# Raw weight pieces in three down products, output steps at a third of the chunks, and six banks for the first scores

## The chip, the cores and the metric

One core of a Trainium2 chip runs the whole program. The metric is device time in microseconds (us), the median of several executions. The profile comes from one further execution that the hardware profiler recorded. Engines are named as in the profile: PE is the matrix engine (TensorE) and PEld its weight loads, DVE is VectorE, ACT is ScalarE, POOL is GpSimd and SP is SyncE. SPq and POOLq are the queues on which SP and POOL issue DMAs.

## The reference, cut to what matters

The input is x of shape (2, 2048, 1024) in float32: 4096 rows of 1024.

```python
x = x + attn(layernorm(x))                # one head of width 256, softmax over 2048 keys
n = layernorm(x)
w = sum of the two largest of n @ gate_w  # one number for each row
h = relu(n @ up_w) ** 2                   # 1024 -> 2048
shared = h @ down_w                       # 2048 -> 1024
routed = (n @ fc1_w @ expert_w * w) @ fc2_w   # 1024 -> 512 -> 512 -> 1024
x = x + layernorm(shared + routed) * gamma + beta
```

Everything is float32. The kernel folds `expert_w @ fc2_w` into one matrix, so that the routed path is a second, narrower pair of products beside up and down.

## The kernel before, in words

**Arithmetic.** Every float32 operand is split into a high and a low part (`fp32r`[...]). One product is then three matmuls: high by high, low by high, high by low (`Pass3`, line 117). A split costs one ACT cast (the high part) and one DVE subtraction (the low part).

**Attention.** The rows are handled in eight blocks n of 512. `scores(n, k)` (line 545) makes one 128 by 512 tile of scores with six matmuls into one PSUM bank, for each of sixteen key chunks k. ACT copies the bank to SBUF (line 557), then DVE takes the running maximum from the same bank (line 562), and after both the bank is free. All scores take their bank from the pool `psb`, which has two. The pool `psa` has four: the query, key and value products before the scores use it, and after them the value products `po` (two banks at a time) and the output projection `pw`. The scores of block 0 stand at the end of the projection stage, where nothing else is left for PE. The following loop runs scores of block n beside the value products of block n-1, `lag` chunks behind. For n = 1 that lag is LAG + 2 = 5, so that five scores of block 1 come ahead of the first value product. A scheduler sets the order of instructions in that part of the program.

**Feed-forward.** From here on the order is written out by hand. The up and down products are done with a fast scheme of seven products in place of eight on half-matrices, for four blocks b of 1024 rows. The products of the down stage run in the order p1, p2, p6, p5, p3, p7, p4 (`DOWN`). Each has NK = 10 chunks, and a chunk takes one weight piece and twelve matmuls. The weight pieces of all stages go through one pipeline, `stage`, `cast_piece`, `end_piece`, seven buffers deep:

- a raw piece is a DMA of 256 KB of float32 (SP, line 808), an ACT cast (line 825) and a DVE subtraction (line 833);
- a kept piece is a DMA of 512 KB of both parts (SP, line 805), with no work for ACT or DVE;
- a piece becomes kept when the split buffer is written to DRAM, 512 KB, by a DMA on POOL (line 836).

The rule is that in block 0 every second piece is written, in block 1 the others are, and a piece that has been written is read back as kept from the next block on. The last LATE = 5 pieces of block 3 are loaded early into other buffers (`load_early`) and have to be kept ones.

The left operand of the down stage goes through a like pipeline (`sum_s`, `cast_s` at line 1062, `end_s` at line 1067, with four buffers `sp`): one ACT cast and one DVE subtraction for each chunk, in every block.

**Output.** A finished row tile y (128 by 1024) goes through `out_step` (line 994), which moves each tile waiting there by one step: load the residual into `res` (SP), add beta to it with a DMA (POOL), take the first moment, then the second moment (ACT), then `write` (two long DVE operations, lines 986 and 987, and the store on POOL, line 988). `out_step` is called by hand: in the up stage after every odd m below 15, in the down stage after every even chunk of p7 and after chunks 0 and 2 of p4. The four tiles that p3 finishes are handled during p7 and p4 of the same block, those that p4 finishes in the next block's up stage. Block 3 handles its own last four tiles at the end.

All engines take their instructions in order, so an instruction that waits holds up all behind it on its engine. In the down stage ACT sees, chunk by chunk, the cast of a weight piece and then the cast of a left operand. DVE sees the two subtractions in the same order, with `write`, the evictions of finished products (lines 1255, 1257, 1259) and the splits of the next block's input (line 150) among them. POOL's queue holds the writes of kept pieces, the stores, the beta additions and the transposed tiles of the next norm.

Of the kernel before, what the change touches and what calls it, by code (L numbers as in the profile page):

```python
# [25 lines left out]
def kernel(  # L26
# [47 lines left out]
    psa = ctx.enter_context(tc.tile_pool(name="psa", bufs=4, space=PSUM))  # L74
    psb = ctx.enter_context(tc.tile_pool(name="psb", bufs=2, space=PSUM))
# [17 lines left out]
    def bank(pool, name):  # L93
        return pool.tile([P, W], FP, tag="b", name=name)
# [259 lines left out]
    NK = (NIC + NLC) // 2  # L354
# [177 lines left out]
        return t  # L532

    st = {}

    def kv_home(j):
        return ex_unit if j < 2 * BPB - 1 else unit
# [7 lines left out]
    def scores(n, k):  # L545
        s = st[n]
        if k % 4 == 0:
            s["s"].append(unit(f"s{n}_{k // 4}", FP))
        pm = bank(psb, "ps")
        acc = Pass3(pm, NDC)  # L550
        kk, q = hl(kv_chunk(n, 0, k)), hl(s["q"])
        for dc in range(NDC):
            acc.add(
                tuple(kk[:, i, ds(dc * W + (k % 4) * P, P)] for i in range(2)),
                tuple(q[:, i, ts(dc, W)] for i in range(2)),
            )
        nc.scalar.copy(s["s"][k // 4][:, ts(k % 4, W)], pm)  # L557
        if k == 0:
            s["max"] = half(f"max{n}")
            nc.scalar.copy(s["max"], pm)  # L560
        else:
            nc.vector.tensor_tensor(s["max"], pm, s["max"], ALU.max)  # L562
# [142 lines left out]

    g_f = half("g_f")[:, : NCC * NE].rearrange("p (c e) -> p c e", c=NCC)
    nc.gpsimd.dma_start(out=g_f, in_=gate_w.rearrange("(c p) e -> p c e", p=P))
    LAG = 3
    xts = []
    for n in range(1, NBLK + 1):  # L710
        if n == NBLK:
# [3 lines left out]
        for k in range(NKC + lag):  # L715
# [7 lines left out]
            if k >= lag:  # L723
                values(n - 1, k - lag)
                if n == BPB and (k - LAG) % 4 == 3:
                    j = BPB + (k - LAG) // 4
# [62 lines left out]
    LATE = 5  # L789
# [5 lines left out]
    def stage():  # L795


        b, s, p, i = pieces.pop(0)
        if len(pieces) < LATE and early:
            staged.append((early.pop(0), False, None))  # L800
            return
        n_w[0] += 1
        w = (wk if n_w[0] % 7 else wv).tile([P, 2 * W], FR, tag="w", name="w")
        if (s, p, i) in kept:
            nc.sync.dma_start(out=w.bitcast(FP), in_=kept[s, p, i])
            staged.append((w, False, None))
            return
        nc.sync.dma_start(out=as_piece(f32(w)[:, W : 2 * W], s), in_=source(s, RIGHT[p], i))

        staged.append((w, True, (s, p, i) if b == 1 or i % 2 == 0 else None))  # L810

    early, n_w = [], [0]

# [146 lines left out]
    class Out:  # L960
# [22 lines left out]
        def write(self):  # L983
            y, rs = self.y, self.m.inverse()
            stt = nc.vector.scalar_tensor_tensor
            stt(y, y, self.m.nm, gamma_sb, ALU.add, ALU.mult)
            stt(y, y, rs, self.res, ALU.mult, ALU.add)
            nc.gpsimd.dma_start(out=of[ds(self.n * W + self.t * P, P), :], in_=y)

    res_pair, todo, loaded, first, second = [], [], [], [], []

    def out_step():

        if second:
            second.pop(0).write()
        if first:
            second.append(first.pop(0))
            second[-1].second()  # L1000
        if loaded:
            first.append(loaded.pop(0))
            first[-1].add_beta()
            first[-1].first()
        if todo:
            loaded.append(Out(*todo.pop(0)))
# [11 lines left out]
    with tc.manual_schedule():  # L1018
        for b in range(NBB):
# [72 lines left out]
            for m, (p, i) in enumerate(UPS[b]):  # L1092
                flush()
                w = next_piece()
                if p != "p2":
                    acc[i] = Pass3(acc_bank("pu"), NCC // 2)
                ps = acc[i].ps
                if p == "p2":
                    acc[i].more()
                for c in range(NCC // 2):  # L1100
                    acc[i].add(piece(w, c, P, slice(0, P)), piece(X[p], c, W, slice(0, W)))
                lat, pair = i >= HU // P, i % 2 and i < HU // P
                c22, c21 = h_at("22", i), h_at("21", i) if m >= 2 * NK else None
                if p == "p1":
                    nc.scalar.copy(c22, ps)
                elif p == "p2":
                    if lat:
                        add(h_at("11", i), ps, rwb[0], ALU.mult)
                    else:
                        relu(h_at("11", i), ps)  # L1110
                        if pair:
                            square(h_at("11", i, 2))
                elif p == "p4":
                    nc.scalar.copy(c21, ps)
                elif p == "p6":
                    add(c22, ps, c22, ALU.subtract)
                    add(c21, c21, c22, ALU.subtract)
                elif p == "p5":
                    add(c22, c22, ps, ALU.add)
                elif p == "p3":  # L1120
                    c12 = h_at("12", i)
                    add(c12, c22, ps, ALU.add)  # L1122
                    if lat:
                        add(c12, c12, rwb[0], ALU.mult)
                    elif pair:
                        relu(h_at("12", i, 2), h_at("12", i, 2))
                        square(h_at("12", i, 2))
                else:
                    add(c21, c21, ps, ALU.add)
                    add(c22, c22, ps, ALU.subtract)  # L1130
                    if lat:
                        add(c21, c21, rwb[1], ALU.mult)
                        add(c22, c22, rwb[1], ALU.mult)
                    elif pair:
                        for v in ("21", "22"):
                            relu(h_at(v, i, 2), h_at(v, i, 2))
                            square(h_at(v, i, 2))

                if m % 2 and m < 15:
                    out_step()  # L1140
                if b == 0 and m in (0, 1, 2, 4, 6, 8, 9, 10, 11, 12, 13):
                    norm2.step()
                if b == 0 and m < NB:
                    split_x(x_t[0], 1, m, X["p2"], split_late)

                m4 = 12 if b == 0 else 10
                if m == m4:
                    x_t[1] = norm2.x
                    X["p4"] = new_x()
                if m > m4 and (m - m4) % 2 and (m - m4) // 2 < NB:  # L1150
                    split_x(x_t[1], 1, (m - m4) // 2, X["p4"], split_late)
                elif m >= 2 * NK and p != "p7":
                    n = {"p4": "p6", "p6": "p5", "p5": "p3", "p3": "p7"}[p]
                    if i == 1:
                        X[n] = new_x()
                    if i % 2 and i < 2 * NB:
                        if p == "p4":
                            sums_x(x_t, i // 2)
                        r_, f_ = PLACE[n]
                        split_x(x_t[r_], f_, i // 2, X[n], split_late)  # L1160

                if (p, i) == ("p1", 0 if b else 4):
                    ga = half("ga")[: 2 * NE, :]
                    nc.scalar.copy(ga, gate_part(X["p1"], 0))
                elif (p, i) == ("p2", 0):
                    gs = half("gs")[: 2 * NE, :]
                    add(gs, ga, gate_part(X["p2"], 1), ALU.add)
                    gt = Gate(gs)
                elif (p, i) == ("p4", 1):
                    add(ga, ga, gate_part(X["p4"], 1), ALU.add)  # L1170
                elif (p, i) == ("p7", 0):
                    add(ga, ga, gate_part(X["p7"], 0), ALU.subtract)
                    gt = Gate(ga)
                if m == 6 or (p, i) == ("p7", 3):
                    gt.largest()
                elif m == 10 or (p, i) == ("p7", 6):
                    rwb[p == "p7"] = gt.spread()
                if p == "p7" and i >= NK - 5:
                    step_s()
# [16 lines left out]
            for j, p in enumerate(("p1", "p2", "p6", "p5", "p3", "p7", "p4")):  # L1196
# [12 lines left out]
                for k in range(NK - late):  # L1209
# [19 lines left out]
                    elif not more and j == 4 and k % 2 == 0 and k < 2 * LATE:  # L1229
                        load_early(k // 2)  # L1230
                        if k < 2 * NB:
                            tiles[k // 2].add_beta()
                    if j == 5 and k % 2 == 0 or j == 6 and k in (0, 2):
                        out_step()
                if late:
                    last_w = [next_piece() for _ in range(late)]
# [5 lines left out]
                for t in range(NB):  # L1242
# [17 lines left out]
                    if late:  # L1260
                        tiles[t].first()
                        tiles[t].second()
                        if t:
                            tiles[t - 1].write()
                if late:
                    tiles[-1].write()
                if p == "p3":
                    ended(0)
                elif p == "p4" and not late:
                    ended(1)  # L1270
            if more:
                t1 = norm1.x
        while todo or loaded or first or second:
            out_step()


# [41 lines left out]
```

## Time and profile before

| | us |
|---|---|
| median of 3 runs | 2368.88 (2367.68 to 2369.89) |
| the profiled execution | 2368.2 |
| its span, first to last instruction | 2366.3 |
| down stage, block 0 (976.62 to 1174.92) | 198.30 |
| down stage, block 1 (1374.92 to 1571.18) | 196.26 |
| down stage, block 2 (1771.18 to 1964.22) | 193.04 |
| down stage, block 3 (2164.22 to the end of its last matmul, 2354.78) | 190.56 |
| first score to first value product (309.99 to 344.73) | 34.74 |

The stage bounds are read off the timeline of PE: the start of the first matmul of a kind to the start of the first of the next. A down stage has 7 products of 10 chunks of 12 matmuls, 840 in all, in every block. The profile's own figure for a matmul (390 ns) overlaps its neighbours, so starts are compared and not sums of durations.

The transfers of the whole program, from the page (kind of transfer, count, size, and the median time from issue to landing):

```profile
w<-w_p SPq DMA_DIRECT2D x350, 512.0 KB, 3.7
w_p<-w POOLq DMA_DIRECT2D x140, 512.0 KB, 4.9
w<-wt SPq DMA_DIRECT2D x210, 256.0 KB, 3.7
```

The first line is the loads of kept pieces, the second the writes that make pieces kept, the third the loads of raw pieces.

### The profile page before, as it was taken

The page shows a single profiled execution, that of the slowest core. Times are in us where ns is not written, and L with a number is a line of the kernel's source. Part 1 is how long each engine was busy: PE and PEld are TensorE (multiplying, and loading weights), DVE is VectorE, ACT ScalarE, POOL GpSimd, SP SyncE. Part 2 cuts the span into 40 slices and gives each one's busy share as a digit, 9 for nine tenths or more (in the row PEclk, how much of TensorE's full clock was granted, in tenths as well). Part 3 has the DMA queues.
Part 4 walks back from the last instruction along what each step waited for, and adds up shares of the span by engine and source line. Part 5 has one row for each costly group of instructions (what it writes and reads, how often), then busy time and mean ns, then how long its engine had stood idle before and what let it go on. Part 6 is the DMA issues. An engine that isn't in the chain of part 4 may idle for free.

```text
span 2366.3 us, 29281 instructions
## 1 busy us (share of the span) xinstructions
PE 2329.5 (98%) x10704; PEld 1918.7 (81%) x10704; DVE 1461.0 (62%) x2168; ACT 1131.6 (48%) x1846; POOL 298.4 (13%) x450
## 2 busy tenths in 40 slices
PE   8999999999999999999999999999999999999998
PEld 7888878888888778888778888878888877888886
DVE  5566559888877565797646567644446562435545
ACT  6555445555544644667452374544055454214224
POOL 3222111011110100111110011210000010000001
PEclk9999999999999999999999999999999999999999
DMA  5977883999997765788996689997557798555595
GB/s 189 322 254 278 285 205 114 290 316 320 283 268 213 258 205 183 236 275 270 313 319 231 234 295 332 323 339 238 192 198 270 254 339 290 195 194 187 200 314 188
DMA packets 225806, 603.98 MB, mean 255 GB/s; under 512 B 18768, under 2 KB 80720, under 8 KB 223616
## 3 DMA queue, kind: packets, MB, share of 16 engines
q1 hardware_dynamic: 152160, 334.02, 40.4%
q0 software_dynamic: 73504, 268.11, 37.0%
q8 instruction: 85, 1.39, 0.2%
q14 instruction: 57, 0.47, 0.1%
HBM read 448.96 MB, written 210.76 MB: 279 GB/s over the span
## 4 chain that ended last, share of the span: by engine, by line
PE 90%; DMA 4%; issue 3%; DVE 2%; ACT 1%; POOL 0%; SPq 0%; POOLq 0%; DVEq 0%; ACTq 0%
PE pu L130 31%; PE pd L130 26%; PE po L130 7%; PE pq L130 7%; PE ps L130 7%; PE pw L130 4%; PE pv L130 4%; PE pg L882 1%; PE pf L130 1%; DMA w<-wt 1%; DMA w<-w_p 1%; DMA res<-in_L_ffn_ln_beta_dram 1%; DMA w_p<-w 1%; PE psum L619 1%; DVE w L833 0%
## 5 line engine op out<-in xcount | busy, mean ns | idle before, releaser
L130 PE MATMUL pd<-w,sp 128*128 128x512 f32 x3336 | 762.4, 390 | 11.3 <-DVE sp L1067 7.2
L130 PEld LDWEIGHTS pd<-w,sp 128*128 128x128 f32 x3336 | 626.0, 188 | 146.5 <-DVE sp L1067 10.3
L130 PE MATMUL pu<-xh,w 128*128 128x512 f32 x2240 | 692.9, 390 | 0.1
L130 PEld LDWEIGHTS pu<-xh,w 128*128 128x128 f32 x2240 | 419.4, 188 | 89.6 <-DVE w L833 1.3
L130 PE MATMUL pu<-xl,w 128*128 128x512 f32 x1120 | 436.2, 389 | 0.9 <-DVE xl L150 0.9
L130 PEld LDWEIGHTS pu<-xl,w 128*128 128x128 f32 x1120 | 210.3, 188 | 45.2 <-DVE xl L150 1.4
L1062 ACT CAST sp<-h 128x512 fp32r<-128x512 f32 x238 | 145.9, 618 | 191.5 <-PE pd L130 159.2
L1067 DVE TENSOR_TENSOR sp<-h,sp 128x512 fp32r<-128x512 f32 x238 | 162.1, 686 | 101.3 <-ACT sp L1062 101.0
L825 ACT CAST w<-w 128x512 fp32r<-128x512 f32 x210 | 128.1, 617 | 174.5 <-DMA w<-wt 158.6
L130 PE MATMUL ps<-q,k 128*128 128x512 f32 x768 | 196.0, 393 | 2.0 <-DVE max L562 1.8
L833 DVE TENSOR_TENSOR w<-w 128x512 fp32r<-128x512 f32 x210 | 143.2, 686 | 82.6 <-ACT w L825 81.6
L130 PE MATMUL po<-p,v 128*128 128x512 f32 x768 | 194.2, 391 | 0.0
L130 PEld LDWEIGHTS ps<-q,k 128*128 128x128 f32 x768 | 142.3, 188 | 36.5 <-DVE max L562 7.3
L130 PEld LDWEIGHTS po<-p,v 128*128 128x128 f32 x768 | 143.1, 188 | 29.2
L150 DVE TENSOR_TENSOR xl<-xt,xh 128x512 fp32r<-128x512 f32 x108 | 74.3, 688 | 130.7 <-ACT xh L149 130.6
L1012 ACT ACTIVATE h<-h 128x1024 f32<-128x1024 f32 x48 | 50.6, 1055 | 209.0 <-DVE h L1122 160.0
L836 POOL DMA_DIRECT2D w_p<-w x140 | 75.2, 537 | 564.0 <-DVE w L833 484.4
L557 ACT COPY s<-ps 128x512 f32<-128x512 f32 x128 | 74.8, 584 | 142.0 <-PE ps L130 141.4
L213 DVE STREAM_TRANSPOSE xblk<-xrow 128x1024 f32<-128x1024 f32 x60 | 121.0, 2016 | 9.6 <-ACT xrow L283 9.6
L562 DVE TENSOR_TENSOR max<-ps,max 128x512 f32<-128x512 f32 x120 | 82.0, 684 | 39.5 <-ACT s L557 39.3
L130 PE MATMUL pq<-xha,w_h 128*128 128x512 f32 x256 | 99.7, 389 | 0.0
L130 PE MATMUL pq<-xha,w_l 128*128 128x512 f32 x256 | 99.7, 389 | 0.0
(181 smaller groups left out, 3027.8 us busy)
## 6 DMA issues: line engine op xcount, KB each, us to landing
w<-w_p SPq DMA_DIRECT2D x350, 512.0 KB, 3.7
w_p<-w POOLq DMA_DIRECT2D x140, 512.0 KB, 4.9
w<-wt SPq DMA_DIRECT2D x210, 256.0 KB, 3.7
xt_d<-xblk POOLq DMA_DIRECT2D x56, 512.0 KB, 4.5
xt<-xt_d POOLq DMA_DIRECT2D x56, 512.0 KB, 6.6
wt<-in_L_ffn_up_w_dram POOLq DMA_DIRECT2D x9, 2048.0 KB, 25.8
wt<-in_L_ffn_down_w_dram POOLq DMA_DIRECT2D x9, 2048.0 KB, 35.2
xres<-in_L_attn_x_dram SPq DMA_DIRECT2D x32, 512.0 KB, 12.8
```

What stands on the lines that cost most here:

```text
L130: nc.tensor.matmul(self.ps, lhsT=a, rhs=b, start=self.i == 0, stop=self.i == self.n - 1, skip_group_check=self.on,)
L150: late_ops.append(lambda: nc.vector.tensor_tensor(lo, t, f32(hi), ALU.subtract))
L213: nc.vector.transpose(b.rearrange("p (q k i) -> p q k i", q=P // SQ, i=SQ), r.rearrange("p (k i q) -> p q k i", k=NCC, i=SQ),)
L557: nc.scalar.copy(s["s"][k // 4][:, ts(k % 4, W)], pm)
L562: nc.vector.tensor_tensor(s["max"], pm, s["max"], ALU.max)
L619: nc.tensor.matmul(pt[:, t : t + 1], lhsT=s["sum"][:, ds(i * W + t * P, P)], rhs=ones, start=i == 0, stop=i == 1,)
L825: nc.scalar.copy(w[:, 0:W], f32(w)[:, W : 2 * W])
L833: nc.vector.tensor_tensor(w[:, W : 2 * W], v[:, W : 2 * W], v[:, 0:W], ALU.subtract)
L836: nc.gpsimd.dma_start(out=kept[key], in_=w.bitcast(FP))
L1012: nc.scalar.activation(o, v, AF.Relu)
L1062: nc.scalar.copy(t[:, 0:W], v)
L1067: add(t[:, W : 2 * W], v, f32(t)[:, 0:W], ALU.subtract)
```

## The change

Three edits, independent of each other.

1. In the down stage the pieces of p3, p7 and p4 are not kept any more: they are loaded raw and split anew in each block. The exception is the last five pieces of p4, which are written once in block 2 and loaded early in block 3, as before.
2. The store of a finished row tile is taken out of `write` and made by `out_step` one step later, so that a tile passes through one step more. In the down stage of blocks 0 to 2 `out_step` is called at every third chunk of p7 and p4 taken together (chunks 0, 3, 6, 9 of p7 and 2, 5, 8 of p4). In block 3 it stays at every second, with chunk 4 of p4 added. In the up stage it is called for odd m below 17.
3. The scores of block 0, and the first five of block 1, take two of every three banks from `psa`, so that they rotate over six.

```diff
-        pm = bank(psb, "ps")
+        wide = n == 0 or n == 1 and k < LAG + 2
+        pm = bank(psa if wide and k % 3 else psb, "ps")
...
-        staged.append((w, True, (s, p, i) if b == 1 or i % 2 == 0 else None))
+        if s == 1 and p in ("p3", "p7", "p4"):
+            keep = b == 2 and p == "p4" and i >= NK - LATE
+        else:
+            keep = b == 1 or i % 2 == 0
+        staged.append((w, True, (s, p, i) if keep else None))
...
             stt(y, y, rs, self.res, ALU.mult, ALU.add)
+
+        def store(self):
+            y = self.y
             nc.gpsimd.dma_start(out=of[ds(self.n * W + self.t * P, P), :], in_=y)
...
+        if written:
+            written.pop(0).store()
         if second:
-            second.pop(0).write()
+            written.append(second.pop(0))
+            written[-1].write()
...
-                if m % 2 and m < 15:
+                if m % 2 and m < 17:
                     out_step()
...
-                    if j == 5 and k % 2 == 0 or j == 6 and k in (0, 2):
+                    if j >= 5 and ((j - 5) * NK + k) % (3 if more else 2) == 0:
                         out_step()
...
                             tiles[t - 1].write()
+                            tiles[t - 1].store()
                 if late:
                     tiles[-1].write()
+                    tiles[-1].store()
...
-        while todo or loaded or first or second:
+        while todo or loaded or first or second or written:
             out_step()
```

Here j is the number of the product in the down stage (5 is p7, 6 is p4), `more` is true in blocks 0 to 2, and `late` in p4 of block 3.

More of the change, by code (lines that the diff above doesn't have):

```diff
@@ L534 @@
     st = {}
+    LAG = 3
     def kv_home(j):
@@ L707 @@
     nc.gpsimd.dma_start(out=g_f, in_=gate_w.rearrange("(c p) e -> p c e", p=P))
-    LAG = 3
     xts = []
@@ L987, in write @@
             stt(y, y, rs, self.res, ALU.mult, ALU.add)
+        def store(self):
+            y = self.y
             nc.gpsimd.dma_start(out=of[ds(self.n * W + self.t * P, P), :], in_=y)
-    res_pair, todo, loaded, first, second = [], [], [], [], []
+    res_pair, todo, loaded, first, second, written = [], [], [], [], [], []
     def out_step():
+        if written:
+            written.pop(0).store()
         if second:
-            second.pop(0).write()
+            written.append(second.pop(0))
+            written[-1].write()
         if first:
```

## The prediction

> **What bounds the kernel now.** The page comes first: PE is busy 98% of the span and PEld 81%, so only PE's gaps and slow stretches can be won. Next the starts of matmuls on PE's timeline. Block 3's down stage runs 840 matmuls in 190.56 us, 0.2269 us each; the quickest stretches show 0.2267 (12 in 2.72 us), so a clean down stage is 840 x 0.2267 = 190.4. Over that, the down stages lose 198.30 - 190.4 = 7.9 in block 0, 5.9 in block 1, 2.6 in block 2 and 0.1 in block 3, 16.5 in all.
>
> The place shows in the table by stretches, here p3, p7 and p4 of the four blocks (after the times each engine's busy us and count, then PE's clock, the DMA share and GB/s), and in PE's timeline of block 0 (start, us, what, idle before):
>
> ```profile
> 1085.60:1174.90 89.30, 84.61 (x362) 68.01 (x361) 67.52 (x103) 55.91 (x105) 18.95 (x31) 0.98 0.93 304
> 1483.90:1571.20 87.30, 82.75 (x361) 67.03 (x361) 58.68 (x88) 48.42 (x91) 18.43 (x30) 1.00 0.97 341
> 1880.20:1964.20 84.00, 81.96 (x360) 67.16 (x359) 50.17 (x73) 42.16 (x78) 10.97 (x16) 1.00 0.91 312
> 2273.20:2354.80 81.60, 81.58 (x360) 67.23 (x359) 42.15 (x60) 35.42 (x68) 6.21 (x9) 1.00 0.71 247
> ...
> 1140.11 4.13 PE L130 MATMUL pd<-w,sp 128*128 128x512 f32 x11 [1.95 <-DVE sp L1067]
> 1144.58 5.95 PE L130 MATMUL pd<-w,sp 128*128 128x512 f32 x25 [0.34 <-DVE y L1257]
> 1151.26 5.76 PE L130 MATMUL pd<-w,sp 128*128 128x512 f32 x24 [0.73 <-DVE sp L1067]
> 1158.69 16.39 PE L130 MATMUL pd<-w,sp 128*128 128x512 f32 x71 [1.68 <-DVE sp L1067]
> ```
>
> The whole loss lies here: 360 matmuls need 81.6 us, and the stretches last 89.3, 87.3, 84.0 and 81.6. Then the waits inside these stretches (total us, times, longest), SP's and ACT's from 1105 to 1172 us for block 0 and SP's from 1510 to 1571 for block 1:
>
> ```profile
> SPq L808 <- DMA w_p<-w: 34.9, 8, 6.8
> ...
> ACT w L825 <- DMA w<-wt: 21.7, 12, 4.0
> ...
> SPq L805 <- DMA w_p<-w: 36.8, 8, 9.1
> ```
>
> SP can't load the next piece because its buffer is still being written to DRAM; so ACT waits for the raw piece, the cast of `sp` stands behind it, and PE waits for `sp`. Block 2 makes no writes; there PE waited 2.0 us for kept loads at a DMA share of 1.04.
>
> The second place is the first scores. From the first score to the first value product PE has 126 matmuls (28.6 us) and two groups of transposes (0.8), but takes 34.74: 5.4 lost. ACT, DVE and PEld show the turn of a bank:
>
> ```profile
> 319.02 0.59 ACT L557 COPY s<-ps 128x512 f32<-128x512 f32 x1 [1.03 <-PE ps L130]
> 319.64 0.69 DVE L562 TENSOR_TENSOR max<-ps,max 128x512 f32<-128x512 f32 x1 [0.93 <-ACT s L557]
> 320.39 1.23 PEld L130 LDWEIGHTS ps<-q,k 128*128 128x128 f32 x6 [0.40 <-DVE max L562]
> ...
> 343.22 1.67 PE L130 MATMUL ps<-q,k 128*128 128x512 f32 x6 [1.36 <-DVE max L562]
> ```
>
> Copy and maximum follow each other on one bank, and with two banks two scores take 3.06 us (weight loads at 318.76 and 321.82) where PE needs 2.72.
>
> **What the Trainium skill says.** "Perfetto Trace Analysis", Identifying the Most-Contended Engine, holds matmul busy time for a bad measure of headroom; the trace agrees: the page's 390 ns a matmul against 227 from start to start. The same page, Matmuls, wants independent groups to rotate through different PSUM banks so that evacuation overlaps the next group; the 3.06 against 2.72 us show what two banks leave uncovered. "DMA: Bandwidth & Descriptors", Issuing engines are not separate DMA queues, says that SP's and POOL's transfers share 16 engines: raw loads land in 3.7 us (median of the program) and in 7.2 in block 1's stretch, beside POOL's writes. "TensorE: Matmul & The Clock Gate", HAM oscillation — how this bites in real kernels, warns that idle PE loses clock, from gaps of about 3.4 us on. Here less was enough: after 1.95 us of idling, 11 matmuls took 4.13 us (clock 0.75 in that slice), some 1.6 us more than 11 x 0.2267. So part of block 0's 7.9 is slow clock, and goes if the gap goes.
>
> **Part 1, raw pieces.** p3, p7 and p4 have 30 pieces a block. Raw before: 30 in block 0, 15 in block 1, none later. After: 30, 30, 30 and 25. So 70 loads of 512 KB become 256 KB, with 70 more ACT casts (0.617 us, 43 us) and 70 more DVE subtractions (0.60 from start to start in a row of them, 42 us). Of the 30 writes, 5 are left, in block 2. The traffic of the three products falls by 15 x 0.52 = 7.9 MB in block 0, by 15 x 0.26 + 7.9 = 11.8 in block 1 (of 29.8: 341 GB/s for 87.3 us), by 7.9 - 2.6 = 5.2 in block 2 and by 6.6 in block 3. That takes the DMA share from above 0.9 to about 0.6 to 0.75, and removes both the writes that hold buffers and most of the queueing.
>
> The price is order. A kept piece has nearly six chunks (16 us) to land. The cast of a raw one stands in ACT's queue ahead of an `sp` that PE needs about four chunks after the piece's load was issued; less some 3 us for casts and subtractions, that leaves an estimated 7 to 8 us. Loads of 3.7 us pass, those of 7.2 do not always. ACT and DVE have room: block 2's DVE goes from 50.2 to 68 us of its stretch (83%), ACT from 42.2 to 61.
>
> **Part 2, output steps.** A `write` holds DVE for 2.6 us (1139.97 to 1142.55). At every second chunk DVE needs, in 5.44 us, 2.6 + 4 subtractions (2.4) + one split (0.6) = 5.6: too much, for four writes and the eviction of p7 (2.4) among them. At every third it is 2.6 + 3.6 + 0.9 = 7.1 of 8.16. Beta has 16 us until `write` in place of 11; it lands in 13.2 here, and DVE waited 2.5 us for it (the 1.68 us gap at 1158.69 lies behind such a wait). The later store frees POOL's queue, which stood 12.2 us before stores. The same 32 stores and residual loads are issued; the eighth step moves one store into the next up stage, where y's buffers are next written at least 73 matmuls (16.5 us) later in program order, which covers a store of 7.4. Cost: nothing. In block 3, steps stay at every second chunk: 2.6 + 2.4 = 5.0 of 5.44, but with p7's eviction 8 chunks need 22.4 of 21.8, which the lead of two chunks covers; without that cover it costs 0.6.
>
> What remains of the 16.5? From below 0.1 a block (block 3 shows it), together 0.4; from above 2.6 a block, what block 2 lost with late loads, together 10.4. DVE at 83% and bursts at the end of p7 speak for something between: I take 1.0 in blocks 0, 1 and 2 and 0.5 in block 3, 3.5. Gain 13.0 (6 to 16).
>
> **Part 3, six banks.** Block 0's scores lose 3.1 of the 5.4, by bank turns alone: gone, as ACT and DVE need 0.6 to 0.7 us a score against 1.36. The other 2.2 lie between block 0's broadcast maximum (338.04) and the first value product. That needs the first `p`, whose low part DVE ends at 345.35, 7.3 us after the maximum and on a DVE without a pause. With one more score ahead of it in the new order (25 matmuls, 5.7 us, and two more before the low part is read) PE waits about 1.0 there: this stall is late next. Gain 4.4; at most 5.4, and 2 if the softmax holds PE further on. The chain begins 3 us earlier, and later `p` have 1 to 3 us to spare against the 1.4 by which PE runs ahead of it; so I take 4.3. The DMA share falls to 0.01 before the feed-forward (720 to 730), so an earlier PE is not stopped by the weight sums.
>
> **Sum.** 2366.3 - 13.0 - 4.3 = 2349.0 of span. The profiled execution was 1.9 above its span, the median 2.6: 2351.6.
>
> **Rivals.**
> 1. The softmax takes back the scores' gain (DVE is busy 31.5 of 32 us from 344 to 376). For: no slack on DVE. Against: its chain starts earlier too. Gain 13.0 + 0.5: 2355.4.
> 2. Order replaces traffic: ACT waits for raw loads, DVE's bursts reach PE, 2.6 in each block. For: block 0 was all raw and lost most. Against: that was beside the writes. Gain 6.1 + 4.3: 2358.5.
> 3. Slower: the raw load's short lead. Block 0 lost 7.9 us on 30 raw pieces, 0.26 each. If that is the price of a raw piece and not of the writes, 115 of them in p3, p7 and p4 of four blocks cost 30.3 against 16.5 now: 13.8 - 4.3 = 9.5 slower, 2378.4. It decides from 0.18 us a piece (20.8 / 115), where landing stays near 7 us. Against: SP's 35 us of waits name the writes.
> 4. Nothing gained: PE's gaps move elsewhere in the stage. 2368.
>
> **How the numbers follow.** My forecast 0.62, rival 1 0.12, rival 2 0.15, rival 3 0.07, rival 4 0.04. A measurement of this kernel can't tell 0.2% (4.7 us) from no change. Forecast and rivals 1 and 2 are faster, less 0.02 of rival 2's edge: 0.87; same 0.06; slower 0.07. The range runs from 16.1 + 5.4 won (2347.4) to the far edge of rival 2, with the scores' low bound, 6.1 + 2 (2360.8).
>
> **What would show it.** Raw loads 280, kept loads 280, writes 115. SP's waits for writes gone from the down stages of blocks 0 and 1; stretches of p3 to p4 near 82.5 us, DMA shares below 0.8; no clock dip. Scores to first value product 30.4 us, with a wait of PE for `p`. Wrong if block 2 or 3 takes longer than now (rival 3: ACT's waits for raw loads stay above 15 us a stretch), or if the value products after the first wait for the softmax.

## The result, and the profile after

The changed kernel takes 2361.06 us (median of 7 runs, 2357.94 to 2364.04) against 2368.88 (7 runs, 2366.40 to 2372.42): a ratio of 0.9968, 95% interval 0.9959 to 0.9978. That is 7.8 us faster. 17.3 were forecast.

The profiled execution of the changed kernel has a span of 2355.8 us and took 2357.94, the quickest of its seven. So the spans differ by 10.5 us where the medians differ by 7.8. PE's timeline, cut at its first score, first row sum, first product of each stage and last product, tells where these 10.5 are. The last column is an experiment that comes below, the changed kernel profiled a second time.

| stretch (us) | before | after | difference | forecast | second profile, difference |
|---|---|---|---|---|---|
| before the first score | 309.99 | 310.49 | +0.5 | 0 | +1.8 |
| first score to first row sum | 72.49 | 68.24 | -4.3 | -4.3 | -4.3 |
| first row sum to first up stage | 371.76 | 373.15 | +1.4 | 0 | +0.7 |
| four up stages | 822.38 | 822.27 | -0.1 | 0 | +1.4 |
| down stage, block 0 | 198.30 | 192.17 | -6.1 | -6.9 | -5.4 |
| down stage, block 1 | 196.26 | 192.31 | -4.0 | -4.9 | -3.5 |
| down stage, block 2 | 193.04 | 192.96 | -0.1 | -1.6 | -0.2 |
| down stage, block 3 | 190.56 | 190.95 | +0.4 | +0.4 | +0.4 |
| after the last product | 11.52 | 13.26 | +1.7 | 0 | +1.7 |
| span | 2366.3 | 2355.8 | -10.5 | -17.3 | -7.5 |

Three rows miss: the down stages won 9.8 instead of 13.0, the end grew by 1.7, and 1.4 were given back between the scores and the feed-forward.

The transfers of the page (kind, queue, count, size, median us to landing) are those that were forecast, and the table by stretches of p3, p7 and p4 shows a smaller DMA share. Its columns are as before: after the times the busy us and counts of PE, PEld, DVE, ACT and POOL, then PE's clock, the DMA share and GB/s.

```profile
w<-w_p SPq DMA_DIRECT2D x280, 512.0 KB, 4.2
w<-wt SPq DMA_DIRECT2D x280, 256.0 KB, 3.4
w_p<-w POOLq DMA_DIRECT2D x115, 512.0 KB, 4.6
```

```profile
1077.20:1166.40 89.20, 88.02 (x389) 72.56 (x388) 69.80 (x107) 57.95 (x109) 11.51 (x17) 1.00 0.74 226
1476.00:1558.70 82.70, 81.06 (x358) 66.76 (x357) 65.84 (x101) 55.20 (x104) 10.98 (x16) 1.00 0.77 238
1868.00:1951.60 83.60, 81.58 (x359) 66.91 (x358) 66.10 (x101) 55.18 (x104) 13.72 (x21) 1.00 0.80 257
2260.00:2342.50 82.50, 82.40 (x363) 67.62 (x361) 56.52 (x83) 46.11 (x89) 6.20 (x9) 1.00 0.54 170
```

Read each line as its length less the count of matmuls times 0.2267 us: 1.0, 1.5, 2.2 and 0.2 us are lost. The DMA share, 0.91 to 0.97 in blocks 0 to 2 before, is now 0.74 to 0.80, and the clock is full. SP's waits (total us, times, longest), from 1105 to 1166 us, name PE where they named writes:

```profile
SPq L810 <- PE pd L130: 43.1, 19, 3.7
SPq L807 <- PE pd L130: 6.8, 3, 2.3
```

So the waits for writes are gone from this part of the stage, and 1.0 to 2.2 us remain in each of blocks 0 to 2 all the same. PE's timeline (start, us, what, idle before) has them as one wait in each of blocks 0, 1 and 2, always at the same line, and the page's row of these matmuls puts all their idle time there:

```profile
1139.15 3.20 PE L130 MATMUL pd<-w,sp 128*128 128x512 f32 x13 [1.18 <-DVE y L1274]
...
1531.40 4.81 PE L130 MATMUL pd<-w,sp 128*128 128x512 f32 x20 [1.64 <-DVE y L1274]
...
1924.34 7.96 PE L130 MATMUL pd<-w,sp 128*128 128x512 f32 x34 [2.02 <-DVE y L1274]
```

```profile
L130 PE MATMUL pd<-w,sp 128*128 128x512 f32 x3336 | 759.0, 389 | 4.9 <-DVE y L1274 4.8
```

L1274 is the eviction of p7: PE can't begin p4 in those banks before DVE has added them to `y`. The timelines of DVE and then of ACT in block 2 show what kept DVE:

```profile
1917.58 0.69 DVE L150 TENSOR_TENSOR xl<-xt,xh 128x512 fp32r<-128x512 f32 x1 [3.52 <-ACT xh L149]
...
1920.94 0.15 DVE L276 RECIPROCAL rs<-sd 128x1 f32<-128x1 f32 x1
1921.01 1.27 DVE L994 SCALAR_TENSOR_TENSOR y<-y,nm,gamma 128x1024 f32<-128x1024 f32 x1
1922.31 1.28 DVE L995 SCALAR_TENSOR_TENSOR y<-y,rs,res 128x1024 f32<-128x1024 f32 x1
1923.51 2.47 DVE L1274 TENSOR_TENSOR y<-y,pd 128x512 f32<-128x512 f32 x4
```

```profile
1912.11 0.62 ACT L833 CAST w<-w 128x512 fp32r<-128x512 f32 x1 [2.57 <-DMA w<-wt]
...
1913.15 1.15 ACT L271 ACTIVATE junk<-y,nm 128x1024 bf16<-128x1024 f32 x1
...
1914.63 1.04 ACT L259 ACTIVATE junk<-y 128x1024 bf16<-128x1024 f32 x1
...
1916.93 0.61 ACT L149 CAST xh<-xt 128x512 fp32r<-128x512 f32 x1
```

The step "at every third chunk" falls on chunks 0, 3, 6 and 9 of p7, and chunk 9 is the last of its ten. So its `write` (L276, L994, L995: 2.6 us) stands directly ahead of the four additions of L1274. DVE idled 3.52 us shortly before, ahead of a split of the next block's input (L150), four more splits and the write. It couldn't use that time: its instructions run in the order of its queue, and the head, the split at L150, was waiting for its cast on ACT (1916.93). ACT had stood 2.57 us behind a raw piece until 1912.11. Then it worked from 1913.15 to 1915.90 on the moments of the output step on chunk 6 (L271, L259), and the casts came after them. Blocks 0 and 1 show the same order, with the same 3.52 us on DVE. So an output step delays the eviction in two ways, through its moments on ACT and through its write on DVE.

### The profile page after: what moved, and what is told of

Read it like the earlier page. It is cut to its first block, busy times and chain, and to the rows that moved or that the text cites. A ratio compares the mean times of both kernels' runs of the same rounds, so it can differ in the third digit from the quotient of the medians.

```text
span 2355.8 us, 29360 instructions
## 1 busy us (share of the span) xinstructions
PE 2323.3 (99%) x10704; PEld 1919.4 (81%) x10704; DVE 1501.8 (64%) x2238; ACT 1168.1 (50%) x1916; POOL 285.4 (12%) x425
## 4 chain that ended last, share of the span: by engine, by line
PE 91%; DMA 3%; issue 3%; DVE 1%; ACT 1%; POOL 0%; SPq 0%; POOLq 0%; DVEq 0%; ACTq 0%
PE pu L130 31%; PE pd L130 28%; PE po L130 7%; PE pq L130 7%; PE ps L130 7%; PE pv L130 4%; PE pw L130 4%; DMA w<-wt 2%; PE pg L890 1%; PE pf L130 1%; PE psum L622 1%; DMA xt<-xt_d 0%; DVE w L841 0%; DMA ew<-in_L_ffn_expert_w_dram 0%; DMA res<-x 0%
## 5 line engine op out<-in xcount | busy, mean ns | idle before, releaser
L841 DVE TENSOR_TENSOR w<-w 128x512 fp32r<-128x512 f32 x280 | 191.6, 687 | 99.0 <-ACT w L833 92.0
L833 ACT CAST w<-w 128x512 fp32r<-128x512 f32 x280 | 170.9, 615 | 166.2 <-DMA w<-wt 155.6
L150 DVE TENSOR_TENSOR xl<-xt,xh 128x512 fp32r<-128x512 f32 x108 | 74.4, 689 | 134.9 <-ACT xh L149 134.9
L844 POOL DMA_DIRECT2D w_p<-w x115 | 61.6, 536 | 508.7 <-DVE w L841 435.0
```

The costliest lines, as they stand in the source:

```text
L150: late_ops.append(lambda: nc.vector.tensor_tensor(lo, t, f32(hi), ALU.subtract))
L833: nc.scalar.copy(w[:, 0:W], f32(w)[:, W : 2 * W])
L841: nc.vector.tensor_tensor(w[:, W : 2 * W], v[:, W : 2 * W], v[:, 0:W], ALU.subtract)
L844: nc.gpsimd.dma_start(out=kept[key], in_=w.bitcast(FP))
```

## The experiments

Ten kernels were run in three groups, each beside the kernel before on its own chip (medians 2369.41, 2369.03 and 2370.21 us). Every ratio below is to that kernel before.

**One part alone, three times.** The first has only the raw pieces, with the old steps and two banks:

```diff
-        staged.append((w, True, (s, p, i) if b == 1 or i % 2 == 0 else None))
+        if s == 1 and p in ("p3", "p7", "p4"):
+            keep = b == 2 and p == "p4" and i >= NK - LATE
+        else:
+            keep = b == 1 or i % 2 == 0
+        staged.append((w, True, (s, p, i) if keep else None))
```

> The kernel before with part 1 alone (raw pieces). Theory A (the writes to DRAM held the buffers): SP's waits for writes vanish in the down stages of blocks 0 and 1, which fall from 198.3 and 196.3 us to about 194 each; block 2 gets dearer (193.0 to about 194.5), because DVE now has the extra subtractions and still a write of an output row at every second chunk; block 3 about 191. Time about 5 us below before. Theory B (the spreading of the output steps made the gain): blocks 0 and 1 stay above 196 and the time is not below before.

The second has only the output steps. The store's later place and the up stage's extra step belong to it, as in the change:

```diff
...
-                    if j == 5 and k % 2 == 0 or j == 6 and k in (0, 2):
+                    if j >= 5 and ((j - 5) * NK + k) % (3 if more else 2) == 0:
                         out_step()
```

> The kernel before with part 2 alone (output steps at every third chunk, stores a step behind). Theory A: the writes of kept pieces still hold the buffers, blocks 0 and 1 stay at about 196 and 195 us, block 2 about 192. Time 3 to 5 us below before. Theory B: blocks 0 and 1 fall below 193.5, as in the changed kernel, and the raw pieces add nothing.

The third has only the banks:

```diff
...
-        pm = bank(psb, "ps")
+        wide = n == 0 or n == 1 and k < LAG + 2
+        pm = bank(psa if wide and k % 3 else psb, "ps")
```

> The kernel before with part 3 alone (six banks). First score to first value product 31.0 us, to the first row sum 68.2 (34.7 and 72.5 before). Theory A (PE reaches the first weights of the feed-forward earlier than their loads): the stretch from there to the first up product grows by about 1.4 us, with a wait of 1.3 us or more near 714, and the time is about 3 us below before. Theory B (that wait in the changed kernel was chance): no such wait, and 4.3 us below before. Down stages as before within 0.5 us each in both.

Measured, with the down stages from the profiles:

| kernel | median, us | ratio (95%) | down stages, blocks 0 to 3 | sum less before | after the last product |
|---|---|---|---|---|---|
| raw pieces alone | 2366.13 | 0.9989 (0.9982 to 0.9995) | 195.54, 192.43, 194.83, 190.96 | -4.4 | 13.23 |
| steps alone | 2365.92 | 0.9979 (0.9968 to 0.9990) | 196.01, 194.56, 190.39, 190.56 | -6.6 | 11.11 |
| banks alone | 2365.73 | 0.9986 (0.9980 to 0.9993) | 198.30, 198.05, 192.51, 190.55 | +1.3 | 11.53 |

No part carries the gain by itself. With the raw pieces alone theory A has the direction right: no wait of SP for writes is left in p3, p7 and p4 of blocks 0 and 1, and block 2 gets dearer. But 5.1 us over 190.4 remain in block 0, and the time falls by 3.3 us where 5 were expected. With the steps alone A holds in blocks 0 and 1, and in the time (3.5 us below). With the banks alone A holds too: the stretch from the first row sum to the first up stage grows by 2.2 us, with a wait of 1.87 us at 717.22. Their first value product and first row sum come 3.7 and 4.3 us earlier. Block 1's down stage is 1.8 us longer there, where 0.5 was allowed; no run shows why.

Look at block 2 of the second kernel, which had no writes of pieces before. Kept pieces with the new steps leave nothing to win (190.39), and DVE waits 2.19 us for PE at p7's eviction; the same steps with raw pieces cost 192.96. So the step on chunk 9 does no harm by itself, but together with the raw pieces' work and waits. This block also corrects a reading of the prediction, which put block 2's loss of 2.6 us on late kept loads. The same kept loads land no sooner here (median 6.5 us in p3, p7 and p4, 6.2 before), at the same DMA share (0.93, 0.91 before), and yet PE doesn't wait. With the old output steps gone, the kept loads by themselves cost PE nothing here.

**The write moved off chunk 9.** The changed kernel, with p7's steps of blocks 0 to 2 at chunks 0, 2, 4 and 7 in place of 0, 3, 6 and 9 (p4's and block 3's stay):

```diff
-                    if j >= 5 and ((j - 5) * NK + k) % (3 if more else 2) == 0:
+                    at = (j - 5) * NK + k
+                    if at in ((0, 2, 4, 7, 12, 15, 18) if more else (0, 2, 4, 6, 8, 10, 12, 14)):
                         out_step()
```

> The changed kernel with the output steps of blocks 0 to 2 at chunks 0, 2, 4, 7 of p7 and 2, 5, 8 of p4, so that no write of an output row stands between the last subtractions of p7 and its eviction. Theory A (that write makes the eviction late): PE's waits for the eviction of p7 (1.2, 1.6 and 2.0 us in the changed kernel) vanish, the down stages of blocks 0 to 2 take about 191 us each, and the time is about 5 us below the changed kernel's, 13 below before. Theory B (the short lead of raw loads leaves DVE too little in hand wherever the write stands): PE waits elsewhere in p7 or p4 instead, the stages stay above 192, and at most 1.5 us are won.

2354.9 us (2354.18 to 2360.54), ratio 0.9939 (0.9925 to 0.9952): 6.2 below the changed kernel's 2361.06, as theory A expected (5). The down stages take 191.06, 191.66, 190.96 and 190.96: 13.5 less than before, where 13.0 were forecast for the change. Of PE's waits for p7's eviction (L1275 in this kernel), 0.56 and 0.29 us are left. The down stages hold 3.7 of the 6.2 us (4.8 against the changed kernel's second profile); where the rest lies, the profiles, each of one execution, don't show. The edit moves the moments on ACT together with the write on DVE, so it doesn't tell apart what each of them is worth.

The profiled run was the slowest of the five: its stretch from first row sum to the up stage took 378.95 us, with PE waiting 2.47 us near 619 for DVE's addition to the attention's output and 1.80 us near 629 for a maximum, and one up stage was 2.1 us longer.

**The weight sums earlier.** On top of that, two steps of the weight sums (sums of half-matrices for the scheme of seven products, made by DMAs during attention) move to attention's block 2, away from the place where PE waited behind a raw load before the feed-forward:

```diff
-            if k in (2, 8) and n > 1 and steps:
+            if k in ((2, 4, 8, 10) if n == 2 else (2, 8)) and n > 1 and steps:
```

> e4_shift with two of the weight-sum steps moved from the last attention blocks to attention block 2 (four steps there in place of two), where the DMA share is near zero around 350 to 395 us. Theory A (what the six banks win at the front is taken back because the DMA-bound weight sums end at a fixed time and the bias additions and first raw loads stand behind them): the stretch from the first row sum to the first up product falls to at most 371.5 us (373.2, 373.9 and 379.0 in the three kernels with six banks, 371.8 to 372.1 in the three with two), PE's waits near 619 and 717 go, and the median is 1.5 to 3 us below e4_shift's 2354.9. Theory B (those waits come from the order of instructions, not from the traffic): the stretch stays above 373 and the median at 2355.

2355.47 us (2353.85 to 2355.76), ratio 0.9939 (0.9926 to 0.9952). By its numbers theory B came out: the stretch from the first row sum to the up stage takes 373.67 us, and the median stays at 2355. Of theory A only the waits came out. PE no longer waits near 619 or 714, and the DMA share from 671 to 700 us is 0.65 where the changed kernel has 1.02. But the same kind of wait (1.91 us, for DVE's maximum) now stands at 569.95, and no time is won over the 2354.9.

**Two banks again.** The kernel with the write moved, without part 3:

```diff
-        wide = n == 0 or n == 1 and k < LAG + 2
-        pm = bank(psa if wide and k % 3 else psb, "ps")
+        pm = bank(psb, "ps")
```

> e4_shift with all scores in two banks again, so parts 1 and 2 with the shifted steps, and without part 3. First score to first row sum 72.5 us, the stretch after it 371.8. Theory A (the banks' 4.3 us are given back in part): the median is only 1 to 3 us above e4_shift's. Theory B (the banks' gain is whole): 4 us or more above it. Down stages as in e4_shift, 191 to 191.7 us.

2360.67 us (2357.68 to 2365.35), ratio 0.9964 (0.9950 to 0.9978). First score to first row sum is 72.52 again. From this pair's medians six banks are worth 5.8 us, as theory B has it (4 or more), with some 3 us of uncertainty in either of them. In the profiles the scores hold 4.3 of it; the down stages (192.14, 191.47, 191.85 and 190.97) are 1.8 longer, and no score is made in those. The profiled run, again the slowest of its kernel, took 378.68 us from first row sum to up stage, not the 371.8 expected. The large wait near 620 us is here too (3.58 us): it doesn't come from six banks.

**The store behind its write.** The kernel with the write moved, and the old order of write and store:

```diff
...
-        if written:
-            written.pop(0).store()
...
-            written.append(second.pop(0))
-            written[-1].write()
+            t = second.pop(0)
+            t.write()
+            t.store()
...
-                if m % 2 and m < 17:
+                if m % 2 and m < 15:
...
-                    if at in ((0, 2, 4, 7, 12, 15, 18) if more else (0, 2, 4, 6, 8, 10, 12, 14)):
+                    if at in ((0, 2, 4, 7, 12, 15, 18) if more else (0, 2, 4, 6, 8, 10, 12)):
```

> e4_shift with the store of an output row made right behind its write, as in the kernel before, and one step less for each tile. Theory A (the later store only frees POOL's queue, on which nothing urgent stands once the kept pieces are no longer written): down stages as in e4_shift within 0.5 us, the median within 2 us. Theory B (the store a step behind is part of the gain): POOL waits for DVE before stores, the transposed tiles of the next norm come late, and the down stages of blocks 0 to 2 take 1 us or more longer each.

2353.62 us (2352.65 to 2355.64), ratio 0.9931 (0.9917 to 0.9946): not slower, as theory A has it, with down stages of 191.42, 190.40, 191.31 and 190.95. The store's later place is worth nothing that shows.

**The changed kernel a second time**, unaltered:

> The changed kernel once more, unaltered, to see which stretches of its profile stand and which vary. Theory A: up and down stages repeat within 0.3 us each (192.2, 192.3, 193.0, 191.0), with the waits for the eviction of p7, and so do the 31.0 and 68.2 us at the scores; the stretch from the first row sum to the first up product varies between 372 and 379. Theory B: the waits for the eviction of p7 are chance and at least one of the three blocks is without them.

2361.35 us (2358.96 to 2366.38), ratio 0.9968 (0.9958 to 0.9978). The waits at L1274 are 1.64, 1.68 and 1.64 us, so they belong to the kernel and not to one execution. The down stages are 192.90, 192.73, 192.86 and 190.95: blocks 0 and 1 repeat within 0.7 and 0.4 us, not within the 0.3 expected, and one up stage is 1.4 longer. The last column of the first table is this profile.

**The last block kept.** The kernel with the store behind its write, where block 2 writes all 30 pieces of p3, p7 and p4, and block 3 loads them kept:

```diff
-            keep = b == 2 and p == "p4" and i >= NK - LATE
+            keep = b == 2
```

> The kernel of e7_store_at_once (six banks, raw pieces, output steps shifted, store behind its write) with one edit: block 2 writes all 30 finished pieces of p3, p7 and p4 (not 5), and block 3 loads them kept (25 loads go from 256 to 512 KB, 25 casts and 25 subtractions leave block 3, 25 writes of 512 KB enter block 2). Open: every kernel with raw pieces in block 3 ends 13.2 to 13.4 us after its last matmul, every kernel without 11.1 to 11.5, and block 3's down stage is 190.95 with raw against 190.56 without. Theory A, the raw pieces of block 3 cause both: tail back to 11.1 to 11.5, block 3 at 190.5 to 190.6, 2.1 us won at the end; block 2's down stage loses less than 2 us by the 25 writes, as block 1 of the kernel with the output steps alone lost 3.2 us with 15 writes and 15 kept loads; net 0 to 2 us faster than e7's 2353.6. Theory B, the tail comes with something else that part 1 brought (the order of the program, not the raw loads): tail stays at 13.2, only block 3's 0.4 goes, and block 2's writes cost what they cost: 1 to 4 us slower than e7. If SP waits for writes (w_p<-w) return in block 2 with over 10 us, block 2's down stage goes above 193.

And beside it the same kernel without this edit:

> The kernel of e7_store_at_once, unaltered, beside e9_keep_last on the same chip, so that the two are compared directly and the quickest version has a second time. If e7's time was no chance: ratio 0.992 to 0.995 to the kernel before, span 2351 to 2355, down stages 191.4, 190.4, 191.3, 191.0 within 0.7 each, tail 13.2 to 13.3, a wait of PE of 0.7 to 2 us behind DVE's maximum near 714 to 718. If it was: span and median near the 2355 of e4 and e5 or above, with PE's waits in the down stages or a longer stretch between the first row sum and the feed-forward.

The second came to 2353.75 us (2352.57 to 2354.29), ratio 0.9934 (0.9922 to 0.9946), down stages 191.16, 190.40, 191.15 and 190.96: as in its first timing. The first took 2359.22 (2356.25 to 2361.38), ratio 0.9957 (0.9945 to 0.9968), 5.5 slower. Theory A holds for the cause and fails for the price. The end fell to 11.27 us and block 3 to 190.56, so the raw pieces of block 3 do cause both. But block 2 rose from 191.15 to 200.50, far past the 2 us that A allowed. The stretch of that stage (columns as before) and SP's waits in it, from 1880 us on, show what 25 more writes do beside raw loads:

```profile
1865.50:1954.50 89.00, 83.25 (x350) 66.86 (x349) 64.57 (x96) 54.87 (x104) 25.37 (x43) 0.96 1.01 360
```

```profile
SPq L810 <- DMA w_p<-w: 34.9, 14, 6.1
SPq L807 <- DMA w_p<-w: 10.2, 5, 7.4
```

The same stretch without these writes, and SP's waits from 1880 us on:

```profile
1866.00:1946.00 80.00, 79.54 (x351) 65.52 (x350) 64.22 (x99) 55.21 (x104) 13.67 (x21) 1.00 0.80 254
```

```profile
SPq L810 <- PE pd L130: 39.7, 18, 3.0
SPq L807 <- DMA w_p<-w: 8.3, 3, 6.0
```

ACT and DVE are as busy in both (64 and 55 us); only the writes differ, 45 us of SP's waits for them against 8, and the stage is 9.3 us longer. About 3 us of that is slow clock, told at the end. This pair prices a raw piece and a write apart, which the prediction could only argue: 25 writes beside raw loads cost 9.3 us, 25 raw pieces in place of kept ones cost block 3 0.4 us and the end 2.0.

Here is DVE's timeline of that quicker kernel at the end of p7 in block 2, to be held against the one of the changed kernel above:

```profile
1909.86 0.69 DVE L841 TENSOR_TENSOR w<-w 128x512 fp32r<-128x512 f32 x1 [3.15 <-ACT w L833]
...
1911.14 1.27 DVE L994 SCALAR_TENSOR_TENSOR y<-y,nm,gamma 128x1024 f32<-128x1024 f32 x1
1912.44 1.29 DVE L995 SCALAR_TENSOR_TENSOR y<-y,rs,res 128x1024 f32<-128x1024 f32 x1
...
1916.92 0.69 DVE L841 TENSOR_TENSOR w<-w 128x512 fp32r<-128x512 f32 x1 [1.36 <-ACT w L833]
1917.53 0.68 DVE L1081 TENSOR_TENSOR sp<-h,sp 128x512 fp32r<-128x512 f32 x1
1918.13 2.47 DVE L1274 TENSOR_TENSOR y<-y,pd 128x512 f32<-128x512 f32 x4
```

DVE waits as before: 3.15 us while ACT stands behind a raw piece, then 1.36 us while ACT works on the moments of a step. But the write has been done two chunks earlier, so when the last splits are done, the eviction follows at once: PE waits 0.46 us here, not 2.02.

## Why the prediction was right or wrong, by its own steps

**Right in the main: what bounded the down stages.** SP's waits for writes vanished from p3, p7 and p4 of blocks 0 and 1, the DMA share of these stretches fell to 0.80 or less, and the clock dip is gone. The pair just shown confirms the reason: writes beside raw loads cost 9.3 us in one stage. The runs of one part alone put beside it that the old output steps held blocks 0 and 1 as well, and block 2 alone.

**Wrong, and the main error: Part 2, "Cost: nothing", and with it "I take 1.0 in blocks 0, 1 and 2".** The working compared sums: 7.1 us of DVE's work in 8.16 us. A sum over three chunks says nothing of the place within them. The steps' places were known from the edit (chunks 0, 3, 6, 9 of p7), and so was the eviction's, right behind chunk 9; block 3 was even worked out with p7's eviction, blocks 0 to 2 were not. The spare time was there, but as idle time ahead of the write, when the head of DVE's queue hung on ACT; the 2.75 us of moments on ACT had no place in the working. The residue measured 1.8, 1.9, 2.6 and 0.5 us over 190.4, 6.8 in all (7.8 in the second profile), where 3.5 were taken. With the write two chunks earlier it is 3.0 (13.5 won of 16.5), and over the five profiles of kernels with these steps and without block 2's extra writes it lies between 2.1 and 4.8. That edit moved other steps of p7 as well, to chunks 2 and 4; the waits at p7's eviction are what ties the gain to the one on chunk 9.

This is half of rival 2's mechanism, "DVE's bursts reach PE", with 1.2 to 2.0 us of waiting in blocks 0 to 2 where it put 2.6 in each block. ACT's waits for raw loads, its other half, reached PE only by way of DVE. The range's lower edge in gain, 2360.8, was this rival's with the scores' low bound; 2361.06 lies just beyond it. The down stages and the scores each gave more than that edge assumes (9.8 and 4.3 against 6.1 and 2), but the end and the middle took back 3.1, and the median keeps 2.7 less of the gain than the profiled span does, as told below.

**Wrong: nothing was set down for the end.** Every kernel with raw pieces in block 3 ends 13.2 to 13.4 us after its last product, every one without 11.1 to 11.5. The forecast costed 25 casts and 25 subtractions in block 3 and left the end as it was. The experiment with the last block kept ties these 1.7 us to block 3's raw pieces. What in them does it stays open; the only trace is SP's wait for PE's queue at the end of the program, in the two kernels of that pair without and with raw pieces in block 3:

```profile
SPq L1333 <- PEq L1333: 0.9, 2, 0.8
```

```profile
SPq L1333 <- PEq L1333: 3.0, 2, 2.5
```

**Wrong by about 1.1 us: "an earlier PE is not stopped by the weight sums".** It rested on a DMA share of 0.01 from 720 to 730 us. The stop comes before: ACT (timeline) stood 5.66 us behind a raw load of the feed-forward's first weights, and the copy of a score stands behind that cast, so PE waited.

```profile
711.90 0.62 ACT L833 CAST w<-w 128x512 fp32r<-128x512 f32 x1 [5.66 <-DMA w<-wt]
712.42 0.58 ACT L560 COPY s<-ps 128x512 f32<-128x512 f32 x1
```

```profile
713.89 1.66 PE L130 MATMUL ps<-q,k 128*128 128x512 f32 x6 [1.49 <-DVE max L565]
```

In the kernel before, these loads are issued from 709.37 on, ahead of the window that the forecast looked at. In the changed kernel the first of them was issued at 705.64, after SP had stood 24.1 us for PE (24.1 in the kernel before too), so the crowded stretch from 671 to 700 us (share 1.02) wasn't what held it: from 700 to 706 the share was 0.15. It landed beside the last bias addition, issued at 704.91, and four more raw loads. ACT's longest wait for these loads is 5.66 us here and 2.63 in the kernel before; what makes that difference isn't shown. Over the profiles, without the two that have the large wait near 620, first row sum to up stage takes 373.0 us with six banks (seven, 371.9 to 373.9) and 371.9 with two (three, 371.8 to 372.1). Moving the weight sums removed the wait at this place and won nothing, and the kernel with the last block kept has six banks, the sums in their old place and no such wait (371.94 us). So it isn't shown that the sums cause the loss.

**Right: the scores.** The first value product comes after 31.02 us (30.4 forecast), the first row sum 4.3 us earlier, as forecast. PE has no gap left up to that product: one more score stands ahead of it, 132 matmuls in place of 126, and 132 x 0.2267 with 0.8 for the transposes is 30.7. The wait for `p` comes behind the first four value products, with 0.60 us where about 1.0 was expected. The softmax didn't take the gain back: rival 1 falls.

**The other rivals.** Rival 3 asked for 0.18 us a raw piece. In the quickest kernel block 1 runs 30 of them, without writes in p3, p7 and p4, in a down stage of 190.40 us: nothing. With the old steps, 30 raw pieces and five writes did cost block 2 1.8 us, 0.06 a piece. ACT's waits for raw loads are 7.1 to 10.6 us a stretch, not above 15. So rival 3 falls, though a sign named for it came, a longer block 3, by 0.4. Rival 4 is not what happened: the idle time on the page's row of these matmuls fell from 11.3 us to 4.9.

**The numbers together.** Of the 9.5 us between forecast and median, the down stages' residue is 3.2, the end 1.7, the middle 1.4 and a later first score 0.5. The rest, 2.7, lies between the profiled execution and the median: that execution took 3.1 us less than its kernel's median, where before's took 0.7 less. What the slower executions spend it on isn't shown. The second profile lies 0.4 below its median, and there an up stage longer by 1.4 (PE waits 1.04 us for the split of a raw weight) and a first score later by 1.8 fill that place; both vary from one execution to the next.

With p7's steps moved alone, the median (2354.9) misses the forecast's 2351.6 by 3.3 us; with the store put back behind its write too, the quickest kernel seen (2353.6 and 2353.8) misses it by 2.

## What to carry to other kernels

Keep a long operation from standing directly ahead of an eviction that the next product waits for. It was harmless here only where the engine came to the eviction with time in hand (2.19 us in block 2 with kept pieces). A sum of work below the time at hand is no reserve if the idle time lies ahead of the operation. Before a step is called hidden, write down the queues around each eviction and bank turn, in order: the engine's own, and that of the engine it waits for. Price a read-back copy by its writes beside other loads (9.3 us for 25 of them in one stage here), not by its own transfers alone.

## What the runs showed of the hardware

The clock dip doesn't follow from the length of one gap. In the kernel before, 1.95 us of idling was followed by 11 matmuls in 4.13 us, at a clock of 0.65 (1140.00 to 1144.20; the prediction's 0.75 is for a slice that it doesn't bound). In the kernel with the banks alone, 2.03 us was followed by a clock of 0.50. But in the changed kernel 2.02 us was followed by 34 matmuls in 7.96, which is full speed (33 x 0.2267, and 0.4 for the last to end), and in the kernel with the steps alone the clock stayed at 1.00 after 2.45 and even after 2.85 us. The DMA share doesn't separate them either: in the 8 us behind the gap it was 0.99 to 1.08 where the clock fell and 1.01 to 1.14 in the kernel with the steps alone. In the experiment with the last block kept, two gaps with a single record between them cost more than themselves, as PE's timeline shows:

```profile
1930.43 0.50 PE L130 MATMUL pd<-w,sp 128*128 128x512 f32 x1 [1.97 <-ACT sp L1076]
1932.88 7.47 PE L130 MATMUL pd<-w,sp 128*128 128x512 f32 x20 [1.95 <-DVE sp L1081]
```

Those 20 take 7.47 us where 4.7 would do, 2.8 us of slow clock (0.50 from 1932.9 to 1937.0). "TensorE: Matmul & The Clock Gate", HAM oscillation — how this bites in real kernels, in the Trainium skill, gives gaps of more than about 3.4 us as the thing to avoid. Here gaps of 1.95 and 2.03 us were enough and one of 2.85 was not. What decides is open.

The other surprise is how far a middle stretch can vary in one and the same place. From 560 to 640 us the DMA share is 1.06 to 1.07, and the four accumulating transfers of 512 KB that add a bias took a median of 33.8 and 35.1 us to land in the two profiles, one with six banks and one with two, in which PE waited 2.5 and 3.6 us for their result. In the nine other profiles with the weight sums in their old place they took 25.3 to 29.3 us, and PE didn't wait there. Single profiles of the stretch from the first row sum to the first up stage differ by 7 us, about as much as the whole change is worth.
